# Due times of the last sequence's chunks, rounding of the last chunk in two halves, and issue costs by kind of transfer, in a planned two-layer transformer kernel

## The chip, the cores and the metric

The kernel runs on one core of one Trainium2 chip. The metric is the device time of one launch in microseconds (us), as the median of several runs. Five engines work side by side on the core: TensorE (PE in the profile; PEld is its weight loads), VectorE (DVE), ScalarE (ACT), GpSimd (POOL) and SyncE (SP), which here does nothing but issue the transfers.

## The reference

The input x has 8 sequences of 1024 rows of 256 float32 numbers. Four blocks follow one another, each added to x after a layernorm of its own:

```
x = x + L0_attn(layernorm(x))   # decoder layer: linear "flow" attention with running sums, 16 heads, then 256 -> 1024 gelu -> 256
x = x + L0_ffn(layernorm(x))    # 256 -> 1024 relu -> 256
x = x + L1_attn(layernorm(x))   # softmax attention, one head of 256, within a sequence of 1024 rows
x = x + L1_ffn(layernorm(x))    # h = silu(q(x) q(Wg).T) * (q(x) q(Wu).T), width 704;  result = q(h) q(Wd).T
```

In the last line q is a rounding to FP4: every 16 neighbouring numbers of a row are divided by a sixth of their largest magnitude, each is rounded to the nearest of 0, 0.5, 1, 1.5, 2, 3, 4 and 6 with its sign, and the result is multiplied back. So the 704 intermediate numbers of a row are rounded in 44 blocks that know nothing of each other.

## The kernel before

**Tiling.** A chunk is 128 rows. A sequence has 8 chunks and there are 64 chunks, numbered 0 to 63. The flow attention works on groups of 4 chunks (16 groups, two to a sequence). `dense` (line 1331) does the two 1024-wide layers half a group at a time, and its weights are loaded anew for each half group into rings of five buffers `w_in` and `w_out`. Softmax attention and the FP4 layer work chunk by chunk, in `soft_chunk` (line 1502). A sequence's soft chunks can begin only when all 8 of its chunks are through the dense layers.

**A planner sets the order.** Every step of the work is a Python generator (a "part") that yields before each piece what this piece needs: its engine, the tiles it reads, how many PSUM banks, a condition `when`, and a due time `at`. `Plan.run` (line 291) goes on with the part that can start soonest by the planner's own clock; among those that are equally ready it takes the one due first. `Plan.took` (line 160) moves that clock: it books a cost for each instruction from its engine, operation and size. What comes out is one fixed order of instructions on each engine. On the chip each engine executes its list in that order and waits on semaphores where data, buffers or banks are not ready. The costs therefore decide only the order.

**Transfers.** All are issued by SyncE. Before the change `took` books 0.4 us for an issue, then the transfer itself at 250 GB/s behind those under way, then 2.1 us until it has landed. Among them are the dense weights (128 KB each), the rows of x, and the pair that lays out a small table over all partitions: two writes to the DRAM tile `packed`, then up to four reads of 256 KB into `spread` tiles (`spread`, line 809).

**Fills.** Where the planner's clock shows TensorE without work for over 1.6 us, `fill` (line 1650) puts matmuls of the identity with itself there (`bank<-ident`, no second operand). They compute nothing that is used; they keep TensorE going.

**A soft chunk.** Its steps on TensorE, in order: the query product with `wqk`; the scores against the whole sequence, two banks of 512 (`n2T,qT`); eight transposes of the probabilities; the product with the values (`vt,probT`); two transposes of the rounded rows (`ident,n`); gate and up products in two column halves of 352 (`wgT`, `wuT`); six transposes of the rounded intermediate rows (on `hid`, or on the former `q` and `k` tiles, which serve as two more such buffers); and the down product (`wdT,hqT`, six matmuls). In between, `fp4` (line 650) rounds the 256-wide rows, and then the 704-wide intermediate rows, in eight VectorE instructions and one on ScalarE (`q_c`). The due time `at` of chunk `cc` is `3.5 + cc / 4`. The transposes of the probabilities are due 0.25 later, those of the rounded rows 0.5 later, and those of the intermediate rows 0.75 later. So before the change the steps of one chunk fall due between those of its neighbours.

The end of a chunk before the change, at lines 1609 to 1620:

```
            yield dve(hid)
            nc.vector.tensor_tensor(hid[:, cols], hid[:, cols], ub, ALU.mult)
        plan.drop(xqT)
        yield dve(hid)
        yield from fp4(hid, INTER)
        hqT = []
        for half in range(2):
            yield pe(hid, banks=1, at=at + 0.75)
```

Of the kernel before, what the change touches and what calls it, by code (L numbers as in the profile page):

```python
# [16 lines left out]
P = 128  # L17
# [5 lines left out]
INTER = 704  # L23
# [12 lines left out]
INTER_TILES = [(t * P, min(P, INTER - t * P)) for t in range((INTER + P - 1) // P)]  # L36
# [26 lines left out]
class Plan:  # L63
# [96 lines left out]
    def took(self, queue, op, args, kw):  # L160

        aps = [x for x in list(args) + list(kw.values()) if isinstance(x, bass.AP)]
        outs = [kw["out"] if "out" in kw else aps[0]]
        if kw.get("accum_out") is not None:
            outs.append(kw["accum_out"])
        size = 1
        for ap in aps:
            n = 1
            for d in ap.shape[1:]:
                n *= d  # L170
            size = max(size, n)

        overlap, after = 0.0, 0.035
        if queue == "tensor":
            size = 1
            for d in outs[0].shape[1:]:
                size *= d
            cost = size * (0.853e-3 if op == "transpose" else 1.687e-3)
            tiled = op == "matmul" and (kw["lhsT"].shape[-1] <= 32 or kw["lhsT"].shape[0] <= 32)
            if tiled or op == "matmul" and kw["lhsT"].dtype == BF16:  # L180
                cost *= 0.25
            if tiled != self.tiled:
                cost += 0.2
            self.tiled = tiled
            after = 0.2
        elif queue == "vector":
            each = {"reciprocal": 6.2e-3, "tensor_tensor_scan": 2.15e-3}.get(op, 1.05e-3)
            cost = 0.17 + each * size
            if op == "tensor_scalar" and outs[0].dtype == BF16:
                cost = 0.16 + 0.26e-3 * size  # L190
            elif op == "scalar_tensor_tensor" and any(ap.shape[-1] == 1 for ap in aps):
                cost += 0.06
            overlap = 0.08
        elif queue == "scalar":
            cost = (0.16 if op == "copy" else 0.26) + 0.82e-3 * size
            for x in args:
                if not isinstance(x, bass.AP) and self.SETS.get(x, self.act_set) != self.act_set:
                    self.act_set = self.SETS[x]
                    self.free[queue] = self.free.get(queue, 0.0) + 1.3
            if kw.get("accum_out") is not None:  # L200
                cost += 0.15
            overlap = 0.1
        elif queue == "gpsimd":
            cost = 0.65 + 0.7e-3 * size
            if op in ("tensor_scalar", "iota"):
                cost = 0.22
            elif op == "memset":
                cost = 0.1 + 0.9e-3 * size
        else:
            cost = 0.4  # L210
        start = self.free.get(queue, 0.0)
        if queue not in ("tensor", "sync"):
            start = max([start] + [self.used.get(ap.tensor.name, 0.0) for ap in outs])
        for ap in aps:
            name = ap.tensor.name
            if self.by.get(name) != queue or queue in ("vector", "gpsimd"):
                start = max(start, self.done.get(name, 0.0) + (0.05 if queue == "gpsimd" else 0.0))
            if name not in self.done and name in self.held:
                start = max(start, self.used[name])
        if queue == "tensor":  # L220
            if start - self.ran > 2.0:
                self.slow = start + 2.1
            if start < self.slow:
                cost *= 2
            self.ran = start + cost
        if queue == "sync":
            start = max(start, self.landed.pop(0))
        end = start + cost
        if queue == "sync":
            n = 4e-6 / 250e-3  # L230
            for d in outs[0].shape:
                n *= d
            self.free["rings"] = max(self.free.get("rings", 0.0), end) + n
            after = self.free["rings"] - end + 2.1
            self.landed.append(end + after)
        self.free[queue] = end - overlap
        for ap in outs:
            self.done[ap.tensor.name] = end + after
            self.by[ap.tensor.name] = queue
        for ap in aps:  # L240
            name = ap.tensor.name
            self.used[name] = max(self.used.get(name, 0.0), end + after)
            if queue != "tensor" and name not in self.kept:
                self.held.discard(name)
# [11 lines left out]
    def pe(self, *tiles, **kw):  # L256
        return self.need("tensor", tiles, **kw)

    def dve(self, *tiles, **kw):
        return self.need("vector", tiles, **kw)  # L260

    def act(self, *tiles, **kw):
        return self.need("scalar", tiles, **kw)
# [92 lines left out]
def block_stack_kernel(ctx: ExitStack, tc: tile.TileContext, a: dict, out: bass.AP):  # L356
# [20 lines left out]
    plan = Plan(tc, tc.nc)  # L377
    nc, pe, dve, act, dma = plan, plan.pe, plan.dve, plan.act, plan.dma
    x_dram = a["L0_attn_inputs"]
    B, L, _ = x_dram.shape  # L380
    NCH = L // P
# [12 lines left out]
    def mm_bank():  # L394
        bank = ps.tile([P, 512], F32, tag="bank", name="bank")
        plan.bank(bank)
        return bank
# [4 lines left out]
    def fresh(kind, need, name=None):  # L402

        need.fresh = kind
        yield need
        return make(kind, name)
# [1095 lines left out]
    def soft_chunk(cc):  # L1502
# [1 line left out]
        g, i = divmod(c, G)  # L1504
        q = seqs[s]
        n2T, vt = q["n2T"], q["vt"]
        at = 3.5 + cc / 4
        yield pe(
            banks=1,
            when=lambda: count["asked"] == cc  # L1510
            and count["asked"] - count["valued"] < (3 if plan.spare else 2),
        )
        bank = mm_bank()
        for e in range(2):
            for k in range(2):
                nc.tensor.matmul(
                    bank[:, e * P : (e + 1) * P],
                    lhsT=wqk[:, k, e * P : (e + 1) * P],
# [10 lines left out]
        banks = []  # L1529
        for kb in range(NG):  # L1530
            yield pe(qT, banks=1)
            bank = mm_bank()
            plan.keep(bank)
            for e in range(2):
                nc.tensor.matmul(
                    bank, lhsT=qT[:, e, :], rhs=n2T[kb][:, e, :], start=e == 0, stop=e == 1
# [9 lines left out]
        prob = []  # L1546
# [9 lines left out]
        for kb in range(NG):  # L1556
            yield pe(prob[kb], banks=1, at=at + 0.25)
            bank = turned([prob[kb][:, j * P : (j + 1) * P] for j in range(G)])
# [9 lines left out]
        bank = mm_bank()  # L1568
        for j in range(NCH):
            nc.tensor.matmul(  # L1570
                bank[:, :D],
                lhsT=probT[j // G][:, j % G, :],
# [13 lines left out]
        bank = turned(halves(n))  # L1586
# [3 lines left out]
        hid = None  # L1590
        for j0 in range(0, INTER, INTER // 2):
            cols = slice(j0, j0 + INTER // 2)
            yield pe(xqT, banks=2)
            gb, ub = mm_bank()[:, : INTER // 2], mm_bank()[:, : INTER // 2]
            for bank, wT in ((gb, wgT), (ub, wuT)):
                for k in range(2):
                    nc.tensor.matmul(
                        bank,
                        lhsT=xqT[:, k, :],
                        rhs=wT[:, k, cols],  # L1600
                        start=k == 0,
                        stop=k == 1,
                    )
            if hid is None:
                hid = yield from fresh("hid", act(gb))
            else:
                yield act(gb)
            nc.scalar.activation(hid[:, cols], gb, AF.Silu)
            yield dve(hid)
            nc.vector.tensor_tensor(hid[:, cols], hid[:, cols], ub, ALU.mult)  # L1610
        plan.drop(xqT)
        yield dve(hid)
        yield from fp4(hid, INTER)
        hqT = []
        for half in range(2):
            yield pe(hid, banks=1, at=at + 0.75)
            tiles = INTER_TILES[4 * half : 4 * half + 4]
            bank = turned([hid[:, f0 : f0 + P] for f0, _ in tiles])
            hqT.append((yield from fresh("prob", act(bank), "hqT")))
            hqT[half] = hqT[half].rearrange("p (k t) -> p k t", k=4)  # L1620
            nc.scalar.copy(hqT[half][:, : len(tiles), :], bank)
        yield pe(*hqT, banks=1)
        bank = mm_bank()
        for k in range(len(INTER_TILES)):
            nc.tensor.matmul(
                bank[:, :D],
                lhsT=hqT[k // 4][:, k % 4, :],
                rhs=wdT[:, k, :],
                start=k == 0,
                stop=k == len(INTER_TILES) - 1,  # L1630
            )
# [6 lines left out]
        nc.sync.dma_start(out=out[s, c * P : (c + 1) * P, :], in_=y)  # L1638
        plan.drop(y)

    def softmax_and_fp4():
        for cc in range(B * NCH):
            q = seqs[cc // NCH]
            yield dve(
                at=3.5 + cc / 4,
                when=lambda: q["normed"] == NCH and cc - count["out"] < (8 if plan.spare else 4) and "softmax" in weights and "ends" in late,
            )
            plan.start(soft_chunk(cc), 3.5 + cc / 4)

    def fill(us):  # L1650

# [52 lines left out]
```

## Time and profile before

| | |
|---|---|
| median of 3 runs | 2649.98 us (2648.61 to 2650.44) |
| profiled execution | 2649.28 us |
| its span, first to last instruction | 2647.6 us |
| TensorE busy | 2610.0 us, 99% |
| VectorE busy | 1927.3 us, 73% |
| ScalarE busy | 1308.1 us, 49% |
| GpSimd busy | 576.9 us, 22% |
| DMA engines, mean busy share of the hardware queue | 27.4% |

The profile is of one execution; 1.7 us of its time lie outside the span. Since every instruction is issued through one helper, all carry line 337, and groups are told apart by the tiles they write and read. A busy TensorE includes the fills.

### The profile page before, as it was taken

The page shows a single profiled execution, that of the slowest core. Times are in us where ns is not written, and L with a number is a line of the kernel's source. Part 1 is how long each engine was busy: PE and PEld are TensorE (multiplying, and loading weights), DVE is VectorE, ACT ScalarE, POOL GpSimd, SP SyncE. Part 2 cuts the span into 40 slices and gives each one's busy share as a digit, 9 for nine tenths or more (in the row PEclk, how much of TensorE's full clock was granted, in tenths as well). Part 3 has the DMA queues.
Part 4 walks back from the last instruction along what each step waited for, and adds up shares of the span by engine and source line. Part 5 has one row for each costly group of instructions (what it writes and reads, how often), then busy time and mean ns, then how long its engine had stood idle before and what let it go on. Part 6 is the DMA issues. An engine that isn't in the chain of part 4 may idle for free.

```text
span 2647.6 us, 46665 instructions
## 1 busy us (share of the span) xinstructions
PE 2610.0 (99%) x16995; PEld 2043.8 (77%) x16995; DVE 1927.3 (73%) x4353; ACT 1308.1 (49%) x2671; POOL 576.9 (22%) x1101
## 2 busy tenths in 40 slices
PE   8999999999999999999999999999999999999999
PEld 7777787877778777787777778777787777777776
DVE  7888786868768586776868678586776867655676
ACT  4534445455464544536455364555536455453443
POOL 2333332212213122131222212122131222111000
PEclk9999999999999999999999999999999999999999
DMA  3435323223132232322323232232322323122000
GB/s 93 124 87 155 99 86 104 77 70 108 56 96 73 76 104 64 92 71 76 90 74 104 63 92 75 73 107 65 88 72 79 91 63 107 55 84 65 14 20 9
DMA packets 286821, 211.96 MB, mean 80 GB/s; under 512 B 24704, under 2 KB 275072, under 8 KB 286592
## 3 DMA queue, kind: packets, MB, share of 16 engines
q1 hardware_dynamic: 286592, 208.97, 27.4%
q8 instruction: 136, 2.23, 0.4%
q14 instruction: 93, 0.76, 0.1%
HBM read 188.17 MB, written 20.71 MB: 79 GB/s over the span
## 4 chain that ended last, share of the span: by engine, by line
PE 86%; DVE 7%; DMA 3%; ACT 3%; issue 1%; POOL 0%; SPq 0%; DVEq 0%; POOLq 0%; ACTq 0%
PE bank L337 86%; DVE prod L337 3%; DMA spread<-packed 2%; ACT L337 1%; DMA packed<-flow 1%; DVE spread L337 1%; DVE hid L337 1%; DVE ln_st L337 0%; ACT prob L337 0%; DVE r L337 0%; DVE u L337 0%; ACT n0T L337 0%; DVE n L337 0%; DVE res L337 0%; DVE ln_mv L337 0%
## 5 line engine op out<-in xcount | busy, mean ns | idle before, releaser
L337 PE MATMUL bank<-half,w_in 128*128 128x256 f32 x2048 | 530.6, 382 | 4.3 <-DMA w_in<-in_L_ffn_w_dram 1.4
L337 PE MATMUL bank<-w_out,hidden 128*128 128x256 f32 x2048 | 532.1, 383 | 0.2 <-ACT hidden L337 0.2
L337 POOL TENSOR_SCALAR ln_ve<-ln_mv 128x1 f32<-128x1 f32 x384 | 97.8, 255 | 1719.3 <-DVE ln_mv L337 1699.9
L337 PEld LDWEIGHTS bank<-w_out,hidden 128*128 128x128 f32 x2048 | 369.5, 190 | 92.7 <-issue 39.6
L337 PEld LDWEIGHTS bank<-half,w_in 128*128 128x128 f32 x2048 | 380.2, 191 | 77.5 <-issue 26.6
L337 ACT ACT_TABLE_LOAD x328 | 420.8, 1283 | 5.9
L337 ACT ACTIVATE hidden<-bank,c_L_ffn_b 128x256 f32<-128x256 f32 x256 | 122.0, 477 | 333.7 <-PE bank L337 333.7
L337 POOL TENSOR_TENSOR ln_rstd<-ln_ve,neghalf 128x1 f32<-128x1 f32 x384 | 237.0, 617 | 31.9
L337 PE MATMUL bank<-n2T,qT 128*128 128x512 f32 x512 | 241.8, 595 | 0.5 <-ACT qT L337 0.5
L337 PE MATMUL bank<-vt,probT 128*128 128x256 f32 x1024 | 231.3, 379 | 0.0
L337 PEld LDWEIGHTS bank<-vt,probT 128*128 128x128 f32 x1024 | 193.3, 190 | 27.0 <-issue 1.0
L337 ACT ACTIVATE hidden<-bank,c_L_attn_b 128x256 f32<-128x256 f32 x256 | 120.5, 471 | 186.7 <-PE bank L337 186.5
L337 DVE TENSOR_TENSOR hid<-hid,bank 128x352 f32<-128x352 f32 x116 | 60.0, 518 | 166.3 <-PE bank L337 138.2
L337 PE MATMUL bank<-wdT,hqT 128*128 128x256 f32 x768 | 176.4, 379 | 1.0 <-ACT hqT L337 1.0
L337 PE MATMUL bank<-wgT,xqT 128*128 128x352 f32 x512 | 172.7, 460 | 0.9 <-ACT xqT L337 0.9
L337 PE MATMUL bank<-wuT,xqT 128*128 128x352 f32 x512 | 172.3, 459 | 0.0
L337 PEld LDWEIGHTS bank<-wdT,hqT 128*128 128x128 f32 x768 | 145.4, 190 | 22.6 <-ACT hqT L337 1.4
L337 DVE TENSOR_TENSOR sc<-bank,triu 128x512 f32<-128x512 f32 x240 | 148.7, 680 | 8.3 <-PE bank L337 7.7
L337 PEld LDWEIGHTS bank<-n2T,qT 128*128 128x128 f32 x512 | 92.0, 190 | 65.9 <-issue 60.0
L337 PEld LDWEIGHTS bank<-wuT,xqT 128*128 128x128 f32 x512 | 97.3, 190 | 54.2
L337 PEld LDWEIGHTS bank<-wgT,xqT 128*128 128x128 f32 x512 | 94.2, 190 | 34.0 <-ACT xqT L337 1.4
L337 DVE TENSOR_REDUCE mx<-bank 128x1 f32<-128x512 f32 x128 | 86.0, 672 | 29.2 <-PE bank L337 29.2
(220 smaller groups left out, 4430.4 us busy)
## 6 DMA issues: line engine op xcount, KB each, us to landing
w_in<-in_L_attn_W_dram SPq DMA_DIRECT2D x256, 128.0 KB
w_out<-in_L_attn_W_dram SPq DMA_DIRECT2D x256, 128.0 KB
w_in<-in_L_ffn_w_dram SPq DMA_DIRECT2D x256, 128.0 KB
w_out<-in_L_ffn_w_dram SPq DMA_DIRECT2D x256, 128.0 KB
spread<-packed SPq DMA_DIRECT2D x90, 256.0 KB
x<-in_L_attn_inputs_dram SPq DMA_DIRECT2D x64, 128.0 KB
xr<-in_L_attn_inputs_dram SPq DMA_DIRECT2D x64, 128.0 KB
rows<-res SPq DMA_DIRECT2D x64, 128.0 KB
```

Of the source, the lines that this page charges most:

```text
L337: ins = method(*args, **kw)
```

## The change

Three things change.

1. `took` books transfers by kind: 0.6 us of issue where an operand has 512 or more elements per partition or the target is `packed`, else 0.38 us; and 2.1 us until landing for the former by size, 1.5 us for the others. No transfer is added, removed or altered.
2. The due times of the last eight chunks (56 to 63, the last sequence) become the same, 17.5, with the same 0.25, 0.5 and 0.75 for the later steps of each.
3. For chunk 63 alone, each column half of the intermediate rows is rounded by a part of its own (`half_rounded`) as soon as gate and up of this half are multiplied; the first two transposes wait only for the first half, the other four for the second, and the down product starts on the first two.

```
-            cost = 0.4
+            spreads = size >= 4 * P
+            cost = 0.6 if spreads or "packed" in outs[0].tensor.name else 0.38
...
-            after = self.free["rings"] - end + 2.1
+            after = self.free["rings"] - end + (2.1 if spreads else 1.5)
...
-        at = 3.5 + cc / 4
+        at = 3.5 + min(cc, B * NCH - 8) / 4
+        alone, rounded = cc >= B * NCH - 1, []
...
+            if alone:
+                plan.start(half_rounded(hid, cols, rounded), at + 0.6)
         plan.drop(xqT)
-        yield dve(hid)
-        yield from fp4(hid, INTER)
+        if not alone:
+            yield dve(hid)
+            yield from fp4(hid, INTER)
         hqT = []
-        for half in range(2):
-            yield pe(hid, banks=1, at=at + 0.75)
-            tiles = INTER_TILES[4 * half : 4 * half + 4]
+        cut = 2 if alone else 4
+        for first, tiles in ((0, INTER_TILES[:cut]), (cut, INTER_TILES[cut:])):
+            yield pe(
+                hid, banks=1, at=at + 0.75, when=lambda: not alone or len(rounded) > bool(first)
+            )
...
-        yield pe(*hqT, banks=1)
+        yield pe(*(hqT[:1] if alone else hqT), banks=1)
         bank = mm_bank()
         for k in range(len(INTER_TILES)):
+            if alone and k == cut:
+                yield pe(hqT[1])
...
+    def half_rounded(hid, cols, rounded):
+        yield dve(hid)
+        yield from fp4(hid[:, cols], INTER // 2)
+        rounded.append(cols)
...
     def softmax_and_fp4():
...
-                at=3.5 + cc / 4,
+                at=3.5 + min(cc, B * NCH - 8) / 4,
...
-            plan.start(soft_chunk(cc), 3.5 + cc / 4)
+            plan.start(soft_chunk(cc), 3.5 + min(cc, B * NCH - 8) / 4)
```

More of the change, by code (lines that the diff above doesn't have):

```diff
@@ L1610, in soft_chunk @@
             nc.vector.tensor_tensor(hid[:, cols], hid[:, cols], ub, ALU.mult)
+            if alone:
+                plan.start(half_rounded(hid, cols, rounded), at + 0.6)
         plan.drop(xqT)
-        yield dve(hid)
-        yield from fp4(hid, INTER)
+        if not alone:
+            yield dve(hid)
+            yield from fp4(hid, INTER)
         hqT = []
-        for half in range(2):
-            yield pe(hid, banks=1, at=at + 0.75)
-            tiles = INTER_TILES[4 * half : 4 * half + 4]
+        cut = 2 if alone else 4
[3 more added lines that the diff above has]
+            )
             bank = turned([hid[:, f0 : f0 + P] for f0, _ in tiles])
-            hqT.append((yield from fresh("prob", act(bank), "hqT")))
-            hqT[half] = hqT[half].rearrange("p (k t) -> p k t", k=4)
-            nc.scalar.copy(hqT[half][:, : len(tiles), :], bank)
-        yield pe(*hqT, banks=1)
+            t = (yield from fresh("prob", act(bank), "hqT")).rearrange("p (k t) -> p k t", k=4)
+            nc.scalar.copy(t[:, : len(tiles), :], bank)
+            hqT.append(t)
+        yield pe(*(hqT[:1] if alone else hqT), banks=1)
         bank = mm_bank()
         for k in range(len(INTER_TILES)):
+            if alone and k == cut:
+                yield pe(hqT[1])
             nc.tensor.matmul(
                 bank[:, :D],
-                lhsT=hqT[k // 4][:, k % 4, :],
+                lhsT=hqT[k // cut if k < cut else 1][:, k % cut if k < cut else k - cut, :],
                 rhs=wdT[:, k, :],
```

## The prediction

> **What bounds the kernel now.** I began with the page's busy times.
>
> ```profile
> span 2647.6 us, 46665 instructions
> PE 2610.0 (99%) x16995; PEld 2043.8 (77%) x16995; DVE 1927.3 (73%) x4353; ACT 1308.1 (49%) x2671; POOL 576.9 (22%) x1101
> ```
>
> TensorE sets the time, so the question is not how busy it is but what its busy time contains and where it pauses. The view by stages comes second (columns: busy us of PE, PEld, DVE, ACT, POOL with instruction counts, granted clock, DMA share, GB/s).
>
> ```profile
> 142.00:144.00 2.00, 0.44 (x2) 0.20 (x2) 1.90 (x8) 0.86 (x3) 1.66 (x5) 1.00 0.19 66
> 144.00:146.00 2.00, 1.02 (x5) 0.79 (x5) 1.93 (x7) 1.61 (x4) 0.88 (x2) 0.77 0.00 0
> 146.00:148.00 2.00, 2.00 (x7) 1.76 (x8) 1.47 (x5) 0.85 (x3) 0.00 (x0) 0.50 0.01 4
> ...
> 260.00:2444.80 2184.80, 2177.75 (x14230) 1707.54 (x14227) 1579.96 (x3531) 1103.60 (x2212) 489.73 (x922) 1.00 0.28 82
> 2444.80:2500.00 55.20, 53.11 (x240) 37.87 (x239) 35.73 (x90) 28.99 (x56) 3.97 (x10) 1.00 0.06 20
> 2500.00:2590.00 90.00, 89.55 (x411) 66.19 (x410) 69.07 (x160) 41.07 (x80) 5.10 (x12) 1.00 0.06 18
> 2590.00:2648.00 58.00, 51.85 (x270) 40.41 (x270) 36.31 (x75) 17.83 (x34) 1.48 (x4) 0.99 0.03 10
> ```
>
> From 260 to 2444.8 us TensorE pauses 7 us in 2185: nothing to win there, something to lose. The last dense matmul (on `w_out`) ends at 2444.8; behind it there are only soft chunks. Third, the timeline of TensorE at the end (start, us, instructions; in brackets the idle time before and its releaser), and fourth, from the groups by form behind 2444.8, the row of the fills (busy us, mean ns).
>
> ```profile
> 2618.99 2.17 PE L337 MATMUL bank<-ident 128*128 128x128 f32 x18
> ...
> 2625.53 1.50 PE L337 MATMUL bank<-ident 128*128 128x128 f32 x12
> ...
> 2631.62 1.35 PE L337 MATMUL bank<-wuT,xqT 128*128 128x352 f32 x4
> 2632.81 7.08 PE L337 MATMUL bank<-ident 128*128 128x128 f32 x62
> 2640.16 0.87 PE L337 MATMUL bank<-ident,hid 128*128 128x128 f32 x6 [0.27 <-DVE hid L337]
> 2641.49 2.86 PE L337 MATMUL bank<-wdT,hqT 128*128 128x256 f32 x12 [0.46 <-ACT hqT L337]
> ```
>
> ```profile
> L337 PE MATMUL bank<-ident 128*128 128x128 f32 x104 | 12.3, 275 | 0.0
> ```
>
> So 12.3 us of the "busy" end are fills: chunk 63 is alone, and TensorE waits 7.2 us while its 704-wide rows are rounded. The 202.8 us from 2444.8 to the span's end divide into 194.5 busy to 2644.4, of them 12.3 fills and **182.2 work**; 5.1 of waits; and 3.2 in which the last sum and its store finish.
>
> **The end, step by step.** Counting in both instruction orders, TensorE has exactly the same matmuls and transposes left behind its last `w_out` matmul, so the 182.2 us stay. What changes is the cover.
>
> *Equal due times.* In the new order the last eight chunks first all go through scores and values, with gate and up products between; their roundings and down products come at the end, side by side. When chunk 63 is being rounded, TensorE still has the down products of chunks 61 and 62. The order after 2444.8 has 7 fills where it had 52. 104 profile records are 52 fills, so one is 12.3/52 = 0.24 us: 1.6 us are left of 12.3.
>
> *Does VectorE become the last to arrive?* I walked the last 56 us of the new order with the durations of this profile, from chunk 59's first gate product, time 0. TensorE has 10 half pairs of gate and up at 2.36 us (steady starts, 2630.44 to 2632.81), one values product at 3.45, 8 down products at 2.59, 62 transposes at 0.11 and the 1.6 of fills: 56.1. VectorE has 88 instructions, 43.5 us by their rows (704-wide 0.89, 352 with bank 0.52, 256 0.42) and 0.03 between each: 46. Taken in order, with the ScalarE `q_c` (0.79; 256-wide 0.42) between, rounded rows are ready and wanted at: chunk 59 25.4 and 33.1; 60 31.5 and 33.6; 61 41.1 and 42.4; 62 44.3 and 45.4; first half of 63 51.9 and 51.3; second half 54.1 and 53.7. Two waits, together 1.1 us. The walk begins with VectorE 3.6 us in, held by a transpose; a backlog beyond 1.1 us would appear one for one.
>
> *Two halves.* No row shows rounding instructions 352 wide within SBUF. They lie between half of 0.89, 0.445, and the 352-wide product out of a bank, 0.52; I took 0.47, nearer to the first since the 704 row has the same operands. Small steps double (0.19 and 0.43 become two of 0.18 and 0.29). Extra VectorE work is 0.3 to 1.1 us, once, and the queue it delays holds only sums `y` of chunks already done. The halves gain little here: in the same walk chunk 63's last up product ends at 45.2, but VectorE reaches its second half only at 46.7, and the last down matmul ends at 57.2. With one 704-wide rounding instead, rows would be ready at 53.5, and six transposes (0.7), a ScalarE copy (0.6) and the six matmuls (2.6) would end at 57.4. So the halves are worth 0.2 us; the cover is worth the rest.
>
> *Waits before that.* Blocks between one query product and the next in the new order have, by the rows, 11.4 to 16 us of TensorE, 10 to 11.9 of VectorE and 5 to 9 of ScalarE, so TensorE bounds them, but narrowly. Before had 2.1 + 0.45 = 2.5 us of waits up to 2590. I keep 2.5; bounds 0.5 and 8, the latter if VectorE reaches only the 0.77 it has from 2500 to 2590 (11.3/0.77 is 1.3 us above a 13.4 us block, six times).
>
> Sum: 182.2 + 1.6 + 1.1 + 2.5 + 3.2 = 190.6 against 202.8: **12.2 us gained** (bounds 6.7 and 14.2).
>
> **Issue costs.** The transfers stay what they are; measured issues are these (min/median/max ns):
>
> ```profile
> L337 SPq DMA_DIRECT2D w_in<-in_L_ffn_w_dram x256: 367/379/1128, 107.9 to 2418.9; - x128
> ```
>
> ```profile
> L337 SPq DMA_DIRECT2D spread<-packed x90: 543/586/1493, 122.0 to 2241.4; - x90
> ```
>
> The new 0.38 and 0.6 fit these. Landing: the trace's landing events, paired with their issues, give `w_in` a median of 1.85 us after the issue, `w_out` 1.70, their slowest tenth over 2.2 to 3.2. The planner now expects 1.5 plus 0.52 of transfer, 2.0, where it expected 2.6: right for most, late for a tenth. [...]
>
> The two orders are identical up to the first `packed` pair near 120 us and differ everywhere after. Up to 2444.8 the new order has 12 more fills, 5 in the pause at 137 and 7 near 190: 2.8 us. Before waits in this stretch: 1.4 for a load at 129.7, 4.3 between 138.6 and 145.4 (0.8, 1.6, 1.0, 0.9), 5.5 from 160 to 260, 7 later. The five fills cover the 0.8. The rest ends on VectorE rounding and layernorms that no edit touches; reshuffled, it may shrink or grow. If all vanished, with the clock loss below, 21 us would go, less 2.8 of fills; if all doubled, 21 would come, plus 2.8. I take +2, nearest to the fills less the 0.8 that they cover, with 6 us either way: the same VectorE work meets the same TensorE work.
>
> [...] The rows above show the clock at 0.50 from about 145 us, and it stays there to 152, some 3 us lost, after four waits of which none exceeds 1.6 us. The same holds for the new order if it pauses there in pieces again: no change. [...]
>
> **Sum.** The profiled execution took 2649.3 us, 0.7 under the median of 2650.0. 2649.3 - 12.2 + 2 = 2639.1; as a median 2639.5.
>
> **Rivals.**
> - *VectorE backlog at the end* (12%). For: 5.1 us of waits at the end come on VectorE and ScalarE results, and gathering eight chunks' roundings in one place leaves it no slack. Against: the walk, with 46 us of VectorE in 56. At the bound, 6.7 gained: 2645.
> - *Loads planned too early* (9%), the slower side. Its place: each of some 30 `packed`/`spread` groups, behind whose 1 MB the dense weights queue. A case stands in the trace: 1.43 us on `w_in` at 129.7 us. For: landing is booked 0.6 earlier. Against: four spreads and two writes are booked 1.2 us later in sum, which offsets that. At 1.43 us each, 7 such waits eat the 10.2 us, 11 make the kernel slower by over 0.2%, and all 30 cost 43. With half of them: 2639.5 + 21.5 = 2661.
> - *The head reshuffles well* (8%): half its waits and the clock loss go, 7 us: 2632.
> - *The change does less than it says* is part of the sum: the halves count 0.2 us, and if gathering the chunks only shifted the fills elsewhere, the order would show them; it has 7 behind 2444.8.
>
> **Chances.** Forecast 71%, own range 2634 to 2645. From this: range 2632 to 2648, which leaves out most of the slower rival and the tails. A measurement here tells 0.2% (5 us) from no change: faster by more needs under 2644.7. Forecast mostly, the good head and half of the backlog give 0.81; same 0.11; slower 0.08.
>
> **What would show it.** Right: behind the last `w_out` matmul about 190 us; fills there under 2 us; no stretch of TensorE over 1 us without work before the last transposes; VectorE's second half of chunk 63 ending some 4 us before the last store begins. Wrong: waits on `DMA w_in` in the dense stretch, a clock under 1 after 260 us, or VectorE results holding TensorE for over 5 us after 2445.

## The result, and the profile after

The changed kernel takes 2660.64 us (median, 2656.63 to 2661.65), the kernel before on the same chip 2649.95 (2648.61 to 2651.26). The ratio is 1.004, with a 95% interval of 1.0027 to 1.0052: **slower by 10.7 us**, where 10 us less were forecast. The profiled execution of the changed kernel took 2658.89 us.

First the head of the page of the kernel after:

```profile
span 2657.2 us, 46512 instructions
PE 2607.8 (98%) x16929; PEld 2034.0 (77%) x16929; DVE 1934.4 (73%) x4361; ACT 1271.5 (48%) x2639; POOL 563.7 (21%) x1101
```

TensorE is busy for 2 us less than before, in a span 9.6 us longer. So, on balance, what was added is time without work. The view by stages of the kernel after says where (columns as before: busy us of PE, PEld, DVE, ACT, POOL with counts, granted clock, DMA share, GB/s):

```profile
0.00:260.00 260.00, 239.57 (x1877) 193.04 (x1878) 206.99 (x504) 116.90 (x290) 75.40 (x154) 0.99 0.41 114
260.00:2471.60 2211.60, 2186.43 (x14227) 1706.25 (x14226) 1587.80 (x3535) 1072.02 (x2183) 479.36 (x924) 1.00 0.28 81
2471.60:2657.20 185.60, 181.79 (x828) 134.67 (x827) 139.63 (x324) 82.57 (x166) 8.91 (x24) 1.00 0.06 18
```

The last `w_out` matmul ends at 2471.6 instead of 2444.8. From there to the end it takes 185.6 us instead of 202.8. The change wins 17.2 us at the end and loses 26.8 in the stretch before it, from 260 us on (the dense stretch), in which the number of matmuls is practically the same (14227 records against 14230). Of the 26.8, TensorE without work makes 18.1 (2211.60 - 2186.43 = 25.2 against 7.0 before), and busy time makes 8.7. The view of waits of the kernel after, for TensorE from 260 to 2471.6 us (total us, times, longest):

```profile
PE bank L338 <- DVE sc L338: 11.2, 9, 2.0
PE bank L338 <- DVE v L338: 9.5, 17, 1.1
PE bank L338 <- DVE kv L338: 1.7, 2, 1.0
...
```

No row of this answer is a load; the four left out are on `res`, `prob`, `n2T` and `e`, 2.5 us in all. Twenty of the 25 us are waits of a matmul into a `bank` for VectorE to write `sc` (the masked scores of the flow attention) or `v`. (A `bank` is one of the eight PSUM banks of the kernel's pool: a matmul writes into it, and the kernel uses it again when another engine has read it.) Before, the same stretch had 0.7 us on `sc` and none on `v`; of its view of waits:

```profile
PE bank L337 <- ACT prob L337: 2.2, 6, 0.6
PE bank L337 <- DVE prod L337: 1.8, 6, 0.5
PE bank L337 <- DVE res L337: 1.2, 1, 1.2
PE bank L337 <- DVE sc L337: 0.7, 1, 0.7
...
```

A matmul that reads `half` and `w_in` does not need `sc` as data. One such place, in the timeline of TensorE of the kernel after (start, us, instructions; in brackets the idle time before and its releaser):

```profile
1179.35 1.03 PE L338 MATMUL bank<-w_out,hidden 128*128 128x256 f32 x4
1180.21 0.38 PE L338 MATMUL bank<-ident,h 128*128 128x128 f32 x2
1182.61 1.13 PE L338 MATMUL bank<-half,w_in 128*128 128x256 f32 x4 [2.02 <-DVE sc L338]
1183.58 0.38 PE L338 MATMUL bank<-ident,hid 128*128 128x128 f32 x2
```

And VectorE at the same time:

```profile
1179.38 0.68 DVE L338 TENSOR_TENSOR sc<-bank,triu 128x512 f32<-128x512 f32 x1
...
1181.87 1.88 DVE L338 TENSOR_TENSOR sc<-bank,triu 128x512 f32<-128x512 f32 x3
```

Between them VectorE works on rows `n` of other chunks. TensorE starts at 1182.61, just after the first of the last three `sc`, which ends near 1182.5. That it waits for the bank which this instruction reads is shown further below. The same wait on `sc`, 2.01 to 2.02 us long, ends at 860.36, 1182.61, 1506.62, 1829.11 and 2151.81: once in each of five sequences, since the planner repeats its pattern from sequence to sequence.

At the very end things are as the prediction wanted them. The timelines of TensorE and, in the last two lines, VectorE of the kernel after:

```profile
2646.22 2.77 PE L338 MATMUL bank<-wdT,hqT 128*128 128x256 f32 x12
...
2649.05 1.73 PE L338 MATMUL bank<-ident 128*128 128x128 f32 x14
...
2651.07 2.89 PE L338 MATMUL bank<-wdT,hqT 128*128 128x256 f32 x12
```

```profile
2649.99 0.53 DVE L338 TENSOR_TENSOR hid<-hid,x_s 128x352 f32<-128x352 f32 x1
2653.99 0.42 DVE L338 TENSOR_TENSOR y<-bank,rows 128x256 f32<-128x256 f32 x1 [3.47 <-PE bank L338]
```

Seven fills (1.73 us) are left of 52, and while the second half of chunk 63 is rounded TensorE has down products of other chunks.

### The profile page after: what moved, and what is told of

The parts are those of the page before. It is cut to its first block, busy times and chain, and to the rows that moved or that the text cites. A ratio compares the mean times of both kernels' runs of the same rounds, so it can differ in the third digit from the quotient of the medians.

```text
span 2657.2 us, 46512 instructions
## 1 busy us (share of the span) xinstructions
PE 2607.8 (98%) x16929; PEld 2034.0 (77%) x16929; DVE 1934.4 (73%) x4361; ACT 1271.5 (48%) x2639; POOL 563.7 (21%) x1101
## 4 chain that ended last, share of the span: by engine, by line
PE 72%; DVE 20%; DMA 3%; ACT 2%; POOL 1%; issue 1%; SPq 0%; DVEq 0%; ACTq 0%; POOLq 0%
PE bank L338 72%; DVE prod L338 3%; DVE hid L338 2%; DVE n L338 2%; DVE ln_st L338 2%; DMA spread<-packed 1%; DVE u L338 1%; DMA packed<-flow 1%; DVE res L338 1%; DVE spread L338 1%; DVE div L338 1%; DVE ln_mv L338 1%; ACT L338 1%; DVE sc L338 1%; DVE mx L338 1%
## 5 line engine op out<-in xcount | busy, mean ns | idle before, releaser
L338 PE MATMUL bank<-half,w_in 128*128 128x256 f32 x2048 | 531.5, 382 | 16.1 <-DVE sc L338 10.7
```

The lines of the kernel that those rows point to most:

```text
L338: ins = method(*args, **kw)
```

## The experiments

### Which of the three edits costs the time

Four kernels ran beside the kernel before (2648.54 us there).

**e1**: the changed kernel with the old booking; due times and halves stay.

```
-            spreads = size >= 4 * P
-            cost = 0.6 if spreads or "packed" in outs[0].tensor.name else 0.38
+            cost = 0.4
...
-            after = self.free["rings"] - end + (2.1 if spreads else 1.5)
+            after = self.free["rings"] - end + 2.1
```

> The changed kernel with transfers booked as before (0.4 us issue, 2.1 us landing), due times and halves kept. Theory A (the new booking of transfers lengthens the dense stretch by about 27 us through waits that come back in every sequence; the due times shorten the end by about 17 us): the last matmul on w_out ends near 2445 us as before, the stretch behind it takes 184 to 190 us instead of 203, time 2632 to 2637 us. Rival B (equal due times or the halves disturb the dense stretch, the booking does not): last w_out near 2470 us, time near 2660 us.

Measured: 2637.72 us (2635.42 to 2638.42), ratio 0.996 (0.9946 to 0.9973).

**e2**: the kernel before with the new booking alone. Against the changed kernel:

```
-        at = 3.5 + min(cc, B * NCH - 8) / 4
-        alone, rounded = cc >= B * NCH - 1, []
+        at = 3.5 + cc / 4
+        alone, rounded = False, []
```

> The kernel before with only the new booking of transfers; due times and rounding as before. Theory A: last w_out near 2471 us, and an end like before's of about 200 us, so 2670 to 2677 us. Rival B: 2648 to 2652 us.

Measured: 2678.77 us (2676.0 to 2682.34), ratio 1.0117 (1.0103 to 1.0131).

**e3**: the kernel before with the equal due times alone.

```
-        at = 3.5 + cc / 4
+        at = 3.5 + min(cc, B * NCH - 8) / 4
```

> The kernel before with only the equal due times of the last eight chunks. Theory A with the prediction's reading of the halves (worth 0.2 us): within 2 us of the version with both, 2632 to 2638 us, no fill behind the last w_out. Rival C (the halves carry a good part of the gain at the end): 5 us or more above the version with both.

Measured: 2636.9 us (2634.54 to 2637.31), ratio 0.9956 (0.9943 to 0.9968).

**e4**: the kernel before with the two halves of chunk 63 alone.

```
+        alone, rounded = cc >= B * NCH - 1, []
...
+            if alone:
+                plan.start(half_rounded(hid, cols, rounded), at + 0.6)
```

> The kernel before with only the halves of chunk 63; due times and booking as before. With nothing left to cover it, chunk 63's rounding stands alone at the end. Theory: the second half's chain (mult 0.52, then eight steps of 0.2 to 0.5, ScalarE 0.43) is about 3 us shorter than the 704-wide one (7.1 us), so 2646 to 2649 us. Rival: the doubled small steps eat it, 2650 us.

Measured: 2648.96 us (2647.41 to 2651.19), ratio 1.0004 (0.9995 to 1.0013). A chain some 3 us shorter was expected from halves alone; the time lies in the range given, but no gain is seen. VectorE takes the steps of both halves in turn: from its last product with a `bank` to the end of the rounding it needs 6.9 us (2632.93 to 2639.80), where the one rounding of the kernel before needs 7.0, and the planner's fills hold TensorE until 2640.92.

The view by stages of e1, then of e2, cut at the end of the last `w_out` matmul (in e2 that matmul ends at 2475.7, 0.4 us before the cut):

```profile
260.00:2444.00 2184.00, 2177.30 (x14226) 1707.23 (x14226) 1579.66 (x3530) 1103.09 (x2212) 489.58 (x922) 1.00 0.28 82
2444.00:2634.50 190.50, 183.15 (x831) 134.85 (x829) 138.93 (x330) 84.38 (x168) 11.60 (x26) 1.00 0.05 17
```

```profile
260.00:2476.10 2216.10, 2191.79 (x14237) 1710.23 (x14236) 1589.62 (x3538) 1073.88 (x2184) 482.96 (x928) 1.00 0.28 81
2476.10:2679.00 202.90, 193.52 (x908) 143.22 (x906) 140.39 (x316) 90.03 (x171) 8.99 (x24) 1.00 0.05 16
```

So the edits fall apart cleanly. The due times win 11.6 us (e3), all behind the last `w_out` matmul. The halves win nothing that can be seen (e1 against e3: +0.8; e4 against before: +0.4). The new booking alone costs 30 us, all before that matmul, although it adds no instruction to speak of and alters no transfer. Of its three figures the 0.6 for `spread` and `packed` does it: the kernel before with the 0.6 alone has on every engine the list of instructions of e2, and with only the 1.5 instead of 2.1 until landing it keeps its own.

### Is it the order, or the banks in which it is executed?

The planner and the kernel disagree in one place. `Plan.bank` reckons that a new bank tile takes the bank that has been free longest by its own clock. But all banks are asked for under one tag from a pool of eight, and the pool chooses by itself. If the pool gives another bank than the planner reckoned with, TensorE waits for whoever still reads it. That is what happens at 1182.61, behind the wait of 2.02 us. On the planner's clock this `half,w_in` starts at 1160.92, in a bank whose `sc` is read out by 1160.27. The built program, which names the bank of every tile, puts it in another one, whose reader is the first of the three `sc` above, planned to end at 1162.45. In the changed kernel 632 of 2464 bank tiles lie elsewhere than the planner reckoned; in the kernel before it is 539 of 2466, with little harm, so the number alone does not tell the cost. Two theories are left: a poor order (waits stay wherever the banks lie), or a fair order in the wrong banks.

**e5**: the changed kernel, each bank tile placed in the bank with which the planner reckons.

```
+    def next_bank(self):   # while free: a new one; else the free one whose use ended first
+        return len(self.banks) if len(self.banks) < BANKS else self.index[self.oldest_bank()]
...
-        bank = ps.tile([P, 512], F32, tag="bank", name="bank")
-        plan.bank(bank)
+        i = plan.next_bank()
+        bank = ps.tile([P, 512], F32, tag=f"bank{i}", name="bank", bufs=1)
+        plan.bank(bank, i)
```

The lists of instructions on all five engines are the same as in the changed kernel; only the banks differ.

> The changed kernel, its instruction order on every engine the same, but each PSUM tile is put in the very bank that the planner reckons with (eight tags of one buffer, picked by the planner's own rule of the bank free the longest) instead of one that the allocator of the eight-buffer pool picks. Theory D (TensorE waits in the dense stretch for VectorE to empty a bank that the planner did not reckon with): the repeating waits on sc (2.02) and v (1.08, 0.64) go, a sequence takes 318 to 319 us instead of 322.3, last w_out near 2446 us, time 2632 to 2640 us. Rival E (VectorE itself is late against the plan, whichever bank): the waits stay, 2657 to 2663 us.

Measured: **2626.48 us** (2626.02 to 2626.71), ratio to the kernel before 0.9917 (0.9903 to 0.993). The view by stages of e5:

```profile
260.00:2439.40 2179.40, 2175.89 (x14225) 1704.73 (x14224) 1586.15 (x3534) 1070.81 (x2182) 478.94 (x923) 1.00 0.28 82
2439.40:2625.00 185.60, 181.81 (x828) 134.68 (x827) 139.65 (x324) 82.58 (x166) 8.91 (x24) 1.00 0.05 18
```

The 25.2 us without work became 3.5, the busy time fell by 10.5, and the end is the same 185.6. The timeline of e5 at the place shown above, TensorE first, then VectorE:

```profile
1169.51 1.03 PE L346 MATMUL bank<-w_out,hidden 128*128 128x256 f32 x4
1170.38 0.38 PE L346 MATMUL bank<-ident,h 128*128 128x128 f32 x2
1170.60 1.03 PE L346 MATMUL bank<-half,w_in 128*128 128x256 f32 x4
1171.46 0.38 PE L346 MATMUL bank<-ident,hid 128*128 128x128 f32 x2
```

```profile
1169.55 0.68 DVE L346 TENSOR_TENSOR sc<-bank,triu 128x512 f32<-128x512 f32 x1
...
1172.04 1.88 DVE L346 TENSOR_TENSOR sc<-bank,triu 128x512 f32<-128x512 f32 x3
```

The same `half,w_in` matmuls now start at once, 1.4 us before the three `sc` begin. Same order, other bank, no wait. Both kernels use all eight; the 32 us of span between them (2657.2 and 2625.0) show that it matters which of the eight comes next.

**Controls for e5.** If pinning banks were good in itself, it would also help the old order. e6 is e3 with the bank edit, e7 the kernel before with it, and e12 is e1 with it:

```
e6:   at = 3.5 + min(cc, B * NCH - 8) / 4     + the bank edit of e5
e7:   the kernel before                       + the bank edit of e5
e12:  cost = 0.4, landing 2.1 (as e1)         + the bank edit of e5
```

> The version with the equal due times only, with the planner's banks. Theory D: the few waits left in its dense stretch (some 4 to 7 us in all) shrink, 2628 to 2636 us. Rival E: 2636 to 2638 us as without.

Measured: 2634.22 us (2632.88 to 2636.28), ratio 0.9948 (0.9936 to 0.996), 2.7 under e3.

> The kernel before with the planner's banks. Theory D: at most the 6 us of waits between 260 and 2445 us and a part of the 5 us at the end can go, 2640 to 2648 us. Rival E: 2648 to 2651 us.

Measured: 2646.87 us (2644.13 to 2648.58), ratio 0.9994 (0.9985 to 1.0003).

> Equal due times and halves with transfers booked as before, with the planner's banks. If the new booking is a gain of its own once the banks agree with the plan: 2631 to 2636 us, 5 us or more above the changed kernel with the planner's banks. If not: 2625 to 2629 us.

Measured: 2633.62 us (2632.6 to 2635.84), ratio 0.9945 (0.993 to 0.996), 4.1 under e1.

The orders of the old booking gain 1 to 4 us, hardly more than these runs tell apart. The order of the new booking gains 34. Whatever else eight tags change beside the bank is in these controls too.

**e11** puts the bank edit on e2, the new booking alone:

```
e11:  at = 3.5 + cc / 4, alone = False, new booking (as e2)     + the bank edit of e5
```

> The new booking of transfers alone, with the planner's banks; due times and rounding as before. Theory D: the dense stretch ends near 2439 us, the end takes some 200 us as without equal due times: 2637 to 2643 us, against 2678.8 with the pool's banks. Rival E: above 2660 us.

Measured: 2644.02 us (2643.11 to 2646.77), ratio 0.9982 (0.9973 to 0.9992): 35 us under e2, and now slightly faster than the kernel before. It is 1 us above the range expected, as e1 and e2 were by 0.7 and 1.8; e5 came out 5.5 us below its range. All four still tell the theories apart.

**e10** leaves the halves out of e5:

```
-        alone, rounded = cc >= B * NCH - 1, []
+        alone, rounded = False, []
```

> The changed kernel with the planner's banks, without the halves of chunk 63. If the halves are worth nothing where other chunks cover the rounding, as the prediction has it (0.2 us): 2625 to 2628 us. If they carry part of the gain: 2629 us or more.

Measured: 2626.7 us (2625.79 to 2628.08), ratio 0.9918 (0.9904 to 0.9933). The halves are worth 0.2 us, which is nothing these runs can tell.

### Another booking between the two

**e8** is the changed kernel with 0.5 instead of 0.6; **e9** is e8 with the bank edit.

```
-            cost = 0.6 if spreads or "packed" in outs[0].tensor.name else 0.38
+            cost = 0.5 if spreads or "packed" in outs[0].tensor.name else 0.38
```

> The changed kernel with 0.5 us instead of 0.6 booked for the issue of a wide transfer. Its order departs from before's only later (after some 930 TensorE instructions instead of 540) and has no fills beyond before's in front of the last w_out. Theory A in its general form (any new order is drawn anew, and what it costs comes back in each of seven sequences): the dense stretch may differ from both by several us times seven at most; if this order happens to repeat before's, 2634 to 2640 us; if it repeats the changed one's waits, 2655 to 2663 us. No value is favoured; it tells whether it is the 0.6 or any departure from 0.4 that does it.

Measured: 2656.49 us (2654.23 to 2657.55), ratio 1.003 (1.0018 to 1.0041). The waits of TensorE of e8 from 250 to 2440 us:

```profile
PE bank L338 <- DVE kv L338: 5.7, 4, 2.2
PE bank L338 <- DVE res L338: 4.1, 5, 1.2
...
```

`v` (3.7) and `hid` (3.5) follow. It is a third order, again with waits for banks, but behind other instructions and at other places than in the changed kernel.

> The version with 0.5 us booked for a wide transfer, with the planner's banks. Theory D, tried on an order that waited elsewhere (kv, res, v, hid instead of sc and v): its waits go as well, a sequence takes 317 to 319 us, last w_out 2438 to 2445 us, time 2626 to 2636 us instead of 2656.5. Rival F (the changed kernel's order was a lucky case for the planner's banks): 2645 us or more.

Measured: 2641.27 us (2639.73 to 2643.27), ratio 0.9973 (0.9963 to 0.9983). The bank edit takes 15 us from e8, but not all of the loss: e9 stays 14.8 us above e5, and above the 2626 to 2636 that were expected. The row of its dense stretch in the stages of e9:

```profile
260.00:2449.60 2189.60, 2179.91 (x14233) 1705.02 (x14233) 1590.84 (x3535) 1079.99 (x2191) 492.92 (x927) 1.00 0.28 82
```

Against e5 its dense stretch has 6.2 us more without work and 4.0 more of busy time, and its end is 4.8 longer (190.4 us). The largest waits left there are on `v`, 2.6 us; what in that order causes them was not tried. With the bank edit, 0.4 (e12), 0.5 (e9) and 0.6 (e5) give 2633.6, 2641.3 and 2626.5 us: the time does not fall step by step as the booking nears the measured issue. Which order the planner falls into decides, and three points do not show that a better booking finds a better one.

## Why the prediction was wrong, and where it was right

- **The end: right in kind, 5 us too little.** Forecast 190.6 us behind the last `w_out` matmul; the changed kernel takes 185.6. The cover came as told, with 1.7 us of fills against 1.6. The walk's waits of 1.1 + 2.5 us did not: 0.5 is left, on `xqT`. The rest is busy time, 181.8 against 183.8; no run shows why. Under the old booking the time is 190.0 (e3) and 190.5 (e1), and as an edit the due times give 11.6 us (e3) where 12.2 were forecast. That the e3 number fits so closely is in part luck: its order has no fills and 5.4 us of waits.
- **The halves: right, as far as can be told.** Forecast 0.2 us; e10 against e5 gives 0.2, not to be told from nothing. A rounding instruction of 352 took 0.52, not the assumed 0.47. The second half of chunk 63 ends at 2650.5, and the last sum, behind which the store follows, at 2654.4: the foretold 4 us.
- **The dense stretch: wrong, and this is the step that failed.** The prediction booked "+2, with 6 us either way", reasoning that "the same VectorE work meets the same TensorE work". It measured +26.8 (e2 alone: +31), more than even the 21 + 2.8 us that it named for all waits doubled and left out of its 6. The premise held: VectorE's busy time there differs by 0.5%. What the step left out are two things. The waits of a new order come back from sequence to sequence, so one unlucky place of 2 us costs 10, and the sum of the waits before is no bound for that. And a matmul needs a bank as well as data; which one it is given the order does not show. e5 shows that second part, with the same order: the waits on `sc` and `v` go, and 32 us of span with them.
- **The head: neutral.** The group of `w_out` matmuls that starts at 288.70 us before starts at 288.87 after. The care that the prediction spent on 120 to 260 us, and its rival of a good head, were spent on the wrong place.
- **The rival on the slower side: right sign, wrong mechanism.** "Loads planned too early" named 2661 us, and 2660.6 was measured, but by accident: after 260 us no row of waits is on a load, and the earlier landing by itself, put into the kernel before, leaves its order as it was. The one wait on `w_out` in the head is 0.9 us.
- **VectorE backlog at the end: did not come.** The waits behind 2471.6 are 0.5 us.
- **Two sums** are off in the last place: the walk's TensorE terms make 56.2 us, not 56.1, and 2639.1 with the 0.7 us makes 2639.8 as a median, not 2639.5. Nothing hangs on either.
- **The clock.** The prediction expected no change where the new order pauses in pieces again. In the stages of the kernel after, by 2 us:

```profile
142.00:144.00 2.00, 1.65 (x8) 1.24 (x7) 1.93 (x7) 1.28 (x4) 1.51 (x3) 0.70 0.00 0
144.00:146.00 2.00, 2.00 (x7) 1.52 (x7) 1.18 (x4) 1.99 (x6) 0.00 (x0) 0.50 0.00 0
...
1184.00:1186.00 2.00, 2.00 (x7) 1.52 (x7) 1.79 (x7) 0.51 (x2) 0.93 (x3) 0.50 0.26 70
1186.00:1188.00 2.00, 2.00 (x10) 1.83 (x9) 0.77 (x3) 1.12 (x3) 1.80 (x4) 0.68 0.22 70
```

In the head the half clock lasts 3.4 us instead of 6.8. In the dense stretch two stretches of 3.4 us are new, at 1184 and 2153, each just behind a 2.02 us wait; the kernel before has none in its dense stretch. At half clock the same work took twice the time (from the start of four `half,w_in` matmuls to that of the next instruction 1.70 us at 143.36, 0.86 at 150.62). So by estimate 3.4 us do the work of 1.7, and the two stretches explain some 3.4 of the 8.7 us by which busy time grew. Part of the remainder is that the matmuls behind a wait show 0.1 us more (1.13 against 1.03 above), some 3 us over 32 waits by estimate; the rest stays open.

**Shown and not shown.** Shown: the new booking costs the time (e1, e2), and of its figures the 0.6 us; the loss comes from the banks in which the new order is executed, since the same order in the planner's banks has none of it (e5, e11); the due times give the gain forecast (e3), the halves none that can be seen (e10). Shown in the built program for the place at 1182.61, not gone through for every wait: that the pool's bank is another than the planner's. By what rule the pool chooses is open, and so is the remainder of e9.

**The best version** is e5, 22 us under the kernel before and 34 under the changed one. Once the banks agree, the new booking itself is a gain: from e12 to e5 it takes 7.1 us by the medians (in the two profiled executions 9.1: some 4 up to the end of the last `w_out` matmul and 5 behind it). Without due times and halves, from e7 to e11, it takes 2.9.

## What to carry to other kernels

Where a planner writes the order, price a change of its costs by what the pattern repeats: look for one place per sequence where an engine could wait, and multiply. Check that the resources which the planner reckons with (which bank, which buffer) are those that the kernel really receives; a matmul that waits on an instruction whose data it does not read is the place to look. And a small correction of a cost, however well measured, can draw another order: try it alone before it is shipped beside edits that are understood.

## What the runs showed of the hardware that was not expected

The length of a wait alone did not tell whether the clock fell. In the kernel after, waits of 1.66, 0.52 and 0.35 us between 138 and 143 us were followed by 3.4 us at half clock. In e5, waits of 1.78, 0.52 and 0.36 us in the same place were not, as its stages show:

```profile
142.00:144.00 2.00, 1.13 (x10) 0.75 (x8) 1.93 (x7) 0.57 (x3) 1.82 (x4) 1.00 0.00 0
144.00:146.00 2.00, 2.00 (x11) 1.35 (x10) 1.90 (x6) 1.97 (x6) 0.37 (x1) 1.00 0.00 0
```

Of the five waits of 2.01 to 2.02 us in the dense stretch of the kernel after, two were followed by half clock and three were not. It began at 1183.87 and 2153.25 us, 1.26 and 1.44 us after the ends of the waits at 1182.61 and 2151.81. Behind those that end at 860.36, 1506.62 and 1829.11 the stages by 2 us show a clock of 1.00 for at least 5 us. Where half clock came it lasted about 3.4 us, or twice that (6.8) in the kernel before. What sets the two kinds of waits apart was not shown: no run moved a wait on purpose to try it.
